# The last linear attention of a four-layer network: chains of taps taken in threes in a fixed order, with the start of a pooled attention beside it

## The chip, the cores and the metric

One core of a Trainium2 chip runs the whole kernel in one launch. The metric is device time in microseconds (us), the median of several executions. One more execution is recorded by the hardware profiler; all durations of single instructions come from that one.

## The reference

The input x is 4 images of 256 channels and 64 x 64 points, in fp32. Four layers follow one another, each `x = x + layer(group_norm(x))`:

```python
# 0: deformable convolution block: 1x1 conv, 3x3 depthwise conv, offsets and masks, bilinear gather of
#    9 points in 4 groups, projection; then squeeze-excite and a feed-forward 256 -> 1024 -> 256
# 1: linear attention
qkv = relu(conv1x1(x, qkv_w) * s + b)                     # 768 channels
agg = depthwise5x5(qkv, agg_dw_w) + ...                   # 25 taps a channel
q, k, v = split(concat([qkv, agg]))                       # in heads of 8
q, k = relu(q), relu(k)
out = (v k^T) q / ((sum k) q + eps)
x = x + relu(conv1x1(out, proj_w) * s + b)
# 2: 3x3 convolution with binarised weights
# 3: attention with keys and values from a 2x2 max pool: softmax(theta^T phi) g, then a 1x1 conv
```

## The kernel before

An image is 2 tiles of 128 channels (KT) by 4096 points, cut into 8 blocks of 512 points (NB). The work is written as Python generators, one for each piece: `feed` (feed-forward), `linear` (layer 1, `layer1`), `conv` (layer 2, `layer2`), `pooled` (layer 3, `layer3`). Each `yield` gives a cost. `beside(steps, number, *works)` runs through a main loop and calls each work so that at every step its spent cost follows a straight line from its share `lo` to its share `hi`; so it writes the instructions of the works interleaved. There are two ways in which that order reaches the engines. Inside `with ordered():` TensorE, VectorE (DVE), ScalarE (ACT) and GpSimd (POOL) get the instructions in the order written. Outside it the framework's scheduler orders them by its own estimates. The DMA queue of SyncE (SP) is left to the scheduler in both.

While the gather of image n runs (`sample`, bound to the four engines in kept order), the feed-forward and linear attention of image n-1 and both last layers of image n-2 go beside it. When the last gather (image 3) is over, three stages are left, all outside `ordered()`:

```python
self.banks, self.alone = cycle(["mm", "acc", "mm", "dp", "mm"]), True
beside(range(64), 64, *behind(N - 1), (conv(N - 2), CONV, 0.2, 1))
self.banks = cycle(["mm", "mm", "mm", "vk"])
beside(range(64), 64, (conv(N - 1, "right"), CONV, 0, 1), (pooled(N - 2, True), SECOND - CONV, 0, 1))
for _ in pooled(N - 1, True): pass
```

`behind(3)` is the feed-forward and then the linear attention of image 3; conv(2) goes beside the latter. Then come conv(3) beside pooled(2), and pooled(3) alone.

**The linear attention.** `rows` makes q, k or v for a block and a tile of channels: a matrix product (L773), ScalarE's relu, and copies into padded buffers (`pad0`, `pad1`) that the 5 x 5 taps read. The tiles are taken in three passes t: two of keys and values, (2, 4) and (3, 5), and one of queries, (0, 1). A chain is 25 taps over 1024 points of one tile; 6 tiles by 4 row groups (NCH) are 24 chains. On VectorE (`depthwise`, L180) each tap is one instruction on an accumulator in PSUM (`agg`). When `alone` is set, chains of which the running number leaves 2 after division by 3 go to `products` instead: ScalarE multiplies (L195, buffers `m`), GpSimd adds (L196). The chains are written one after the other. After every third tap `step` takes one piece from the list `later`: the relu of a finished chain, the transposes and outer products of keys and values (`outer`), the sums over keys (`summed`, kk), and for queries the output: `dens` (denominator, rd), `head` (num, rden, ot; eight for each row group), `proj` (ps, pr, xq; four).

**PSUM** has eight banks of 512 fp32 columns: three `mm`, one each of `acc`, `dp` and `vk`, two of `agg`. `ps()` hands them out in the turn that `banks` says.

**layer2** adds 18 products (36 TensorE instructions, L937) for each block and tile of channels, yields after each three, and adds the result to x (`leave`, L928) after the first three of the next such unit. **layer3** has a preamble over 8 blocks (L988 to L1005) and then 32 iterations, four to a block: scores s (L1022), their maxima (L1023), exponentials (L1029), transposes (L1037, L1038), the product with the values (L1042), scaling (L1043). With `wide` the scores take banks of acc, dp and agg.

Of the kernel before, what the change touches and what calls it, by code (L numbers as in the profile page):

```python
# [9 lines left out]
F32 = mybir.dt.float32  # L10
# [7 lines left out]
P = 128  # L18
N, C, H, W = 4, 256, 64, 64
# [7 lines left out]
NCH = NT // CT  # L27
# [7 lines left out]
LEADS = 12, 14, 16, 18  # L35
# [3 lines left out]

CONVOLVE, OFFSETS, BINARY = NB * 9 + 26, 60, 62  # L40
FEED = NB * 40 + 8
LINEAR = 930
CONV, SECOND = NB * 32 + 2, 631
EPS_BN = 1e-5
EPS_GN = 1e-5
# [25 lines left out]
class Net:  # L71
# [10 lines left out]
    def ps(self, name="ps"):  # L82

        tag = next(self.banks)
        return (self.mm if tag == "mm" else self.ps1).tile([P, 512], F32, name=name, tag=tag)

    def rsqrt(self, pool, v, eps, cols, name):

# [82 lines left out]
    def depthwise(self, acc, src, w, k, rows, cols, r0, bias=None, step=lambda cost: cost, out=None):  # L171


        nc = self.nc
        for t in range(k * k):
            s = src[:, r0 + t // k:r0 + t // k + rows, t % k:t % k + cols]
            wt = w[:, t:t + 1]
            if t:
                to = acc if out is None or t < k * k - 1 else out
                nc.vector.scalar_tensor_tensor(to, s, wt, acc, ALU.mult, ALU.add)  # L180
            elif bias is not None:
                nc.vector.tensor_scalar(acc, s, wt, bias, ALU.mult, ALU.add)
            else:
                nc.vector.tensor_scalar(acc, s, wt, None, ALU.mult)
            if t % 3 == 2 or t == k * k - 1:
                yield step(3.9)

    def products(self, pool, acc, src, w, k, rows, cols, r0, bias, step):

        nc = self.nc  # L190
        for t in range(k * k):
            s = src[:, r0 + t // k:r0 + t // k + rows, t % k:t % k + cols]
            if t:
                m = pool.tile([P, rows, cols], F32, name="m", tag="product", bufs=4)
                nc.scalar.activation(m, s, AF.Copy, scale=w[:, t:t + 1])  # L195
                nc.gpsimd.tensor_tensor(acc, acc, m, ALU.add)  # L196
            else:
                nc.scalar.activation(acc, s, AF.Identity, bias=bias, scale=w[:, t:t + 1])
            if t % 3 == 2 or t == k * k - 1:
                yield step(0.5)  # L200


    def setup(self):
# [514 lines left out]
    def layer1(self, n, st, st2):  # L718
        nc, tc, a = self.nc, self.tc, self.a
        rw = lambda v: v.rearrange("p (r w) -> p r w", w=W)  # L720
        fl = lambda v: v.rearrange("p r w -> p (r w)")
        with tc.tile_pool(name=f"la{n}", bufs=1, side="right") as sp, \
# [11 lines left out]
            ld = sp.tile([P, 4, 64], F32, name="ld")  # L734
            nc.vector.memset(ld, 0.0)

            later, turn, count = [], 0, 0
            room = lambda bufs: bufs + self.alone

            def step(cost, chains=False):  # L740


                nonlocal count
                if later:
                    later.pop(0)()
                if chains:
                    count += 1
                    if count in LEADS:
                        next(made, None)
                return cost  # L750


# [2 lines left out]
            ks = [sp.tile([P, 2, NB], F32, name=f"ks{t}") for t in range(2)]  # L755
            ready = []

            def rows():


                for t, tiles in enumerate(((2, 4), (3, 5), (0, 1))):
                    new = lambda c: [self.padded(bp, 1, 20, 2, c, f"pad{i}", bufs=room(3)) for i in range(2)]
                    pads = {0: new(0)}
                    for b in range(NB):
                        c, h = divmod(b, 2)
                        x = self.block(bp, self.x3_d[n], b, "xr")
                        if h and c + 1 < NCH:
                            pads[c + 1] = new(c + 1)
                        got = []
                        for i, m in enumerate(tiles):  # L770
                            ps = self.ps()
                            for k in range(KT):
                                nc.tensor.matmul(ps, qw[:, k, m * P:(m + 1) * P], x[:, k], start=k == 0, stop=k == KT - 1)  # L773
                            bn = {"bias": qb[:, m:m + 1], "scale": self.vec("qkv_s", m)}
                            dst = {j: p[i][:, 0] for j, p in pads.items()}
                            if t < 2:
                                v = bp.tile([P, 512], F32, name="v", tag=f"v{i}")
                                added = {} if i else {"accum_out": ks[t][:, 0, b:b + 1]}
                                nc.scalar.activation(v, ps, AF.Relu, **bn, **added)  # L779
                                self.spread(dst, rw(v), b, 2)  # L780
                                got.append(v)
                            else:
                                self.spread(dst, None, b, 2, lambda own: nc.scalar.activation(own, rw(ps), AF.Relu, **bn))  # L783
                            if i:
                                if got:
                                    outer(t, 0, *got, t == 0 and b == 0, False)
                                for j in [c - 1] * (b > 0 and not h) + [c] * (b == NB - 1):
                                    ready.append((t, tiles, j, [p[:, 0] for p in pads.pop(j)]))
                            yield

            def aggregate(pd, i, name, relu=True, **more):


                nonlocal turn
                turn += 1
                v = lambda tag, bufs: bp.tile([P, 16, W], F32, name=name, tag=tag, bufs=bufs)
                tick = lambda cost: step(cost, True)
                if self.alone and turn % 3 == 2:
                    out = v("av2", 3)
                    yield from self.products(bp, out, pd, self.w5[:, i], 5, 16, W, 0, self.b5[:, i:i + 1], tick)  # L800
                else:
                    acc, out = self.ps1.tile([P, 16, W], F32, name="agg", tag="agg"), v("ag", room(3))
                    yield from self.depthwise(acc, pd, self.w5[:, i], 5, 16, W, 0, bias=self.b5[:, i:i + 1], step=tick, out=out)
                if relu:
                    later.append(lambda: nc.scalar.activation(out, out, AF.Relu, **more))
                return out

            def outer(t, kind, kv, vv, first, last):

# [74 lines left out]
                for h in range(2):  # L884
                    later.extend([partial(head, h, j) for j in range(4)] + [partial(proj, h, m) for m in range(KT)])

            made = rows()
            for _ in range(3 * NCH):
                while not ready:
                    next(made)  # L890
                    yield step(3)
                t, tiles, c, pd = ready.pop(0)
                count, got = 0, []
                for i, m in enumerate(tiles):
                    more = {} if t == 2 or i else {"accum_out": ks[t][:, 1, c:c + 1]}
                    got.append((yield from aggregate(pd[i], m, ("ak", "av")[i], t == 2 or not i, **more)))
                if t == 2:
                    output(c, pd, got)
                    continue
                outer(t, 1, *map(fl, got), False, c == NCH - 1)  # L900
                if c == NCH - 1:
                    later.append(partial(summed, t))
            while later:
                yield step(4)

# [1 line left out]
    def layer2(self, n, st, st3, side="left"):  # L907
        nc, tc = self.nc, self.tc
        with tc.tile_pool(name=f"ca{n}", bufs=1, side=side) as sp, \
# [5 lines left out]
            for b in range(NB):  # L915
# [15 lines left out]
                        nc.sync.dma_start(self.x5_d[n][:, :, b * 512:(b + 1) * 512], xv)  # L931

                for m in range(KT):
                    ps = self.ps()
                    for i in range(KT * 9):
                        k, t = i // 9, i % 9
                        nc.tensor.matmul(ps, w[:, k, t, m * P:(m + 1) * P], xp[:, k, t // 3:t // 3 + 8, t % 3:t % 3 + W],  # L937
                                         start=i == 0, stop=i == KT * 9 - 1)
                        if i % 3 == 2:
                            if before:  # L940
                                before.pop()()
                            yield 2.7
                    before.append(partial(leave, m, ps, xv, b))
# [109 lines left out]
    def run(self):  # L1053
# [11 lines left out]
        def second(n):  # L1065
            yield from conv(n)
            yield from pooled(n)

        def beside(steps, number, *works):
# [14 lines left out]

            for i, _ in enumerate(steps, 1):
                advance(i / number)
            while open_:
                advance(float("inf"))

        rounds = sum(-(-n_ // RP) for _, n_ in BLOCKS)  # L1090
        E = mybir.EngineType
# [2 lines left out]
        with self.tc.tile_pool(name="gather", bufs=2, side="left") as self.gp, \  # L1094
# [16 lines left out]
            with ordered():  # L1111
                beside(self.sample(1, ssum[1]), rounds, (self.binarise(), BINARY, 0, 0.2), *behind(0))
                for n in range(2, N):
                    beside(self.sample(n, ssum[n]), rounds, *behind(n - 1), (second(n - 2), SECOND, 0.2, 1))
        self.banks, self.alone = cycle(["mm", "acc", "mm", "dp", "mm"]), True
        beside(range(64), 64, *behind(N - 1), (conv(N - 2), CONV, 0.2, 1))

        self.banks = cycle(["mm", "mm", "mm", "vk"])
        beside(range(64), 64, (conv(N - 1, "right"), CONV, 0, 1), (pooled(N - 2, True), SECOND - CONV, 0, 1))
        for _ in pooled(N - 1, True):  # L1120
            pass

# [92 lines left out]
```

## Time and profile before

| | us |
|---|---|
| median of 3 runs | 9327.45 (9320.3 to 9335.84) |
| the profiled execution: its own time | 9288.0 |
| its span (first to last instruction) | 9285.9 |
| feed-forward of image 3 ends (last statistics on VectorE) | 7700.6 |
| first tap of the last linear attention | 7720.6 |
| its last tap | 8513 |
| its last store issued | 8564.9 |
| last product of conv(3) ends | 9079 |

| busy over the span | us | share | instructions |
|---|---|---|---|
| TensorE, products | 6286.0 | 68% | 35252 |
| VectorE | 5026.0 | 54% | 6119 |
| ScalarE | 2188.6 | 24% | 4879 |
| GpSimd | 5063.8 | 55% | 4886 |

The shares are means over stages with different limits. What the change touches lies in the last 1800 us, so the windows there are to be read and not these shares. In the profile's rows a group is named by its line, engine and operation, then output <- inputs; behind the bar stand its busy time, the mean ns of one, the idle time of the engine just before it, and what ended it.

### The profile page before, as it was taken

Reading aid. Unit: us, or ns where it says so; the run is one execution under the profiler, and the core shown is the slowest. Engines: PE = TensorE matmul, PEld = TensorE weight load, DVE = VectorE, ACT = ScalarE, POOL = GpSimd, SP = SyncE. Lnnn points to the kernel's source line nnn. Section 1 sums busy time; section 2 is a strip of 40 time slices with the busy share of each in tenths; the row PEclk is TensorE's granted clock in tenths of the full one; section 3 lists DMA queues with packets and bytes.
Section 4 is the critical chain, followed back from the end, with each engine's and each line's share of the span. In section 5 each row is a group of like instructions: output and inputs, shape, how many; then the busy total and the mean of one; then the engine's idle time right before and its main releaser. Section 6 shows DMA issues by size and latency. Waiting matters only on the chain. (4 is left out here: it accounts for less than half of the span.)

```text
span 9285.9 us, 93043 instructions
## 1 busy us (share of the span) xinstructions
PE 6286.0 (68%) x35252; PEld 3432.4 (37%) x35252; DVE 5026.0 (54%) x6119; ACT 2188.6 (24%) x4879; POOL 5063.8 (55%) x4886
## 2 busy tenths in 40 slices
PE   4354544458544557888876877878768796548999
PEld 2232232234323222344444443434444443323556
DVE  4444443443467677226777762266777625775224
ACT  1111111112211111222222222222222225532224
POOL 1666666566666666666666555666665505742000
PEclk7676666669766677999988889999888898778999
DMA  6455554444433344444443435444433321101211
GB/s 162 125 156 148 141 165 126 129 143 146 136 106 104 111 120 115 139 134 125 125 130 112 120 111 153 130 125 124 133 110 116 104 86 45 33 28 57 62 47 62
DMA packets 819967, 1054.96 MB, mean 114 GB/s; under 512 B 464320, under 2 KB 524864, under 8 KB 817984
## 3 DMA queue, kind: packets, MB, share of 16 engines
q0 software_dynamic: 225024, 614.77, 23.0%
q1 hardware_dynamic: 594496, 434.25, 16.4%
q8 instruction: 279, 4.57, 0.2%
q14 instruction: 168, 1.38, 0.0%
HBM read 880.72 MB, written 167.90 MB: 113 GB/s over the span
## 5 line engine op out<-in xcount | busy, mean ns | idle before, releaser
L579 POOL DMA_INDIRECT g<-tab,sl x4688 | 4610.4, 983 | 2798.2 <-issue 1226.2
L180 DVE SCALAR_TENSOR_TENSOR agg<-pad,vec,agg 128x1024 f32<-128x1024 f32 x2280 | 2934.7, 1287 | 64.9
L586 PE MATMUL acc<-g,wm 128*32 128x128 f32 x18752 | 1011.5, 330 | 2006.7 <-ACT at L591 1362.5
L586 PEld LDWEIGHTS acc<-g,wm 128*32 128x32 f32 x18752 | 553.6, 126 | 2514.4 <-ACT at L591 1564.0
L937 PE MATMUL ps<-xp,w 128*128 128x512 f32 x2304 | 1104.7, 619 | 54.0 <-ACT xp L925 23.8
L570 DVE TENSOR_TENSOR wm<-con,sl 128x1024 f32<-128x1024 f32 (+1 forms) x296 | 358.3, 1211 | 814.2 <-remote 560.9
L611 ACT COPY dT<-dp 64x112 f32<-64x112 f32 x1176 | 286.3, 243 | 1554.5 <-remote 695.8
L937 PEld LDWEIGHTS ps<-xp,w 128*128 128x128 f32 x2304 | 436.9, 198 | 542.6 <-issue 501.8
L704 PE MATMUL ps<-x2f,f 128*128 128x512 f32 x1024 | 506.4, 645 | 8.0 <-ACT f L695 4.0
L169 DVE SCALAR_TENSOR_TENSOR hm<-ps,vec,lk 128x512 f32<-128x512 f32 x256 | 191.0, 751 | 505.9 <-ACT lk L168 411.6
L711 PE MATMUL ps<-hm,f 128*128 128x512 f32 x1024 | 458.5, 602 | 0.0
L773 PE MATMUL ps<-xr,qw 128*128 128x512 f32 x768 | 444.5, 706 | 19.7 <-ACT v L779 11.4
L196 POOL TENSOR_TENSOR av<-av,m 128x1024 f32<-128x1024 f32 x96 | 226.1, 2355 | 409.4 <-DMA xr<-x 320.3
L591 ACT COPY at<-acc 128x256 f32<-128x256 f32 (+1 forms) x588 | 218.3, 371 | 690.1 <-remote 551.5
L619 PE MATMUL po<-dT,ow 128*128 128x224 f32 (+1 forms) x1216 | 321.4, 413 | 66.8 <-issue 32.6
L819 ACT COPY kt<-pt 128x512 f32<-128x512 f32 x256 | 147.8, 585 | 841.7 <-remote 486.8
L196 POOL TENSOR_TENSOR ak<-ak,m 128x1024 f32<-128x1024 f32 x96 | 226.6, 2361 | 181.8 <-ACT m L195 174.6
L168 ACT ACTIVATE lk<-ps,low 128x512 f32<-128x512 f32 x256 | 174.4, 687 | 628.6 <-PE ps L704 461.6
L619 PEld LDWEIGHTS po<-dT,ow 128*128 128x128 f32 x1216 | 261.8, 229 | 131.2 <-issue 80.2
L1022 PE MATMUL s<-ph,th 128*128 128x512 f32 x512 | 281.7, 653 | 30.6 <-ACT pad L783 15.1
L704 PEld LDWEIGHTS ps<-x2f,f 128*128 128x128 f32 x1024 | 201.8, 205 | 258.5 <-issue 241.4
L1042 PEld LDWEIGHTS ps<-gt,pT 128*128 128x128 f32 x2048 | 268.7, 207 | 70.2 <-issue 47.2
(233 smaller groups left out, 7709.1 us busy)
## 6 DMA issues: line engine op xcount, KB each, us to landing
g<-tab,sl POOLq DMA_INDIRECT x4688
x<-x SPq DMA_DIRECT2D x128, 512.0 KB
xr<-x SPq DMA_DIRECT2D x96, 512.0 KB
x<-in_x SPq DMA_DIRECT2D x64, 512.0 KB
tab<-xo SPq DMA_DIRECT2D x512, 64.0 KB
y<-yc SPq DMA_DIRECT2D x32, 512.0 KB
x2f<-x SPq DMA_DIRECT2D x32, 512.0 KB
xyf<-x SPq DMA_DIRECT2D x32, 512.0 KB
```

The source lines that it names most:

```text
L180: nc.vector.scalar_tensor_tensor(to, s, wt, acc, ALU.mult, ALU.add)
L196: nc.gpsimd.tensor_tensor(acc, acc, m, ALU.add)
L570: nc.vector.tensor_tensor(wm[:, 0:nu], self.con("own").unsqueeze(1).unsqueeze(1).to_broadcast(sh), sl[:, r:r + nu, G:].unsqueeze(3).to_bro ...
L579: nc.gpsimd.indirect_dma_start(out=g[:, i, :], out_offset=None, in_=table, in_offset=bass.IndirectOffsetOnAxis(ap=sl.bitcast(I32)[:, r, i: ...
L586: nc.tensor.matmul(acc[32 * i:32 * i + 32, :], wm[:, r4, 4 * i + 2 * x:4 * i + 2 * x + 2, :], g[:, i, x * P:(x + 1) * P], start=x == 0, st ...
L611: nc.scalar.copy(dT[b][hs, :, q0:q0 + m * (v1 - v0)].rearrange("p g (v o) -> p g v o", o=m), dp[u][hs, v0:v1, :, s, 0:m].rearrange("p v g ...
L619: nc.tensor.matmul(po[m][:, 0:np_], self.ow[:, k, m * P:(m + 1) * P], dT[b][:, k, 0:np_], start=k == 0, stop=k == G - 1)
L704: nc.tensor.matmul(ps, f1[:, k, m * P:(m + 1) * P], x2[:, k], start=k == 0, stop=k == KT - 1)
L711: nc.tensor.matmul(ps, f2[:, k, m * P:(m + 1) * P], hm[:, k], start=k == 0, stop=k == 4 * KT - 1)
L773: nc.tensor.matmul(ps, qw[:, k, m * P:(m + 1) * P], x[:, k], start=k == 0, stop=k == KT - 1)
L937: nc.tensor.matmul(ps, w[:, k, t, m * P:(m + 1) * P], xp[:, k, t // 3:t // 3 + 8, t % 3:t % 3 + W], start=i == 0, stop=i == KT * 9 - 1)
L1022: nc.tensor.matmul(s[i], tv[:, 4 * b + j], ph[:, i * 512:(i + 1) * 512], start=True, stop=True)
```

## The change

It leaves the arithmetic as it is. It sets the stages behind the last gather anew:

- The feed-forward and the linear attention of image 3 go into `ordered()`, with 900 steps in place of 64. Beside the linear attention goes `rest`, which is conv(2) and behind it pooled(2) in one generator, at a pace that would end at share 1.46. What is left of it at share 1 (a cost of 240 of 631) goes beside conv(3), outside `ordered()` as before.
- Chains are taken in threes: first and third on VectorE, the second on ScalarE and GpSimd, advanced by one product after every second tap of the others. A tap is one step. `later` gives a piece on every second tap, `rows` one block and tile on every eighth.
- The padded buffers are five for each name instead of four, the buffers `m` three instead of four.
- `banks` stays at `mm` alone (three banks in turn); the units of layer2 take acc and dp in turn (`long`). pooled(2) is no longer `wide`; pooled(3) still is.
- A unit of layer2 leaves after nine products of the next one (i = 8) while `alone` is set.

The core of the diff:

```diff
+    def long(self):
+        return self.ps1.tile([P, 512], F32, name="ps", tag=next(self.idle)) if self.alone else self.ps()
...
-            if t % 3 == 2 or t == k * k - 1:
-                yield step(3.9)
+            if self.alone or t % 3 == 2 or t == k * k - 1:
+                yield step(1.3 if self.alone else 3.9)
...
-                m = pool.tile([P, rows, cols], F32, name="m", tag="product", bufs=4)
+                m = pool.tile([P, rows, cols], F32, name="m", tag="product", bufs=3)
...
-            if t % 3 == 2 or t == k * k - 1:
-                yield step(0.5)
+            yield step(0.5)
...
             def step(cost, chains=False):
                 nonlocal count
-                if later:
+                count += chains
+                if later and (not self.alone or count % 2 or not chains):
                     later.pop(0)()
                 if chains:
-                    count += 1
-                    if count in LEADS:
+                    if count % 8 == 6 if self.alone else count in LEADS:
                         next(made, None)
+                    if count % 2 and aside:
+                        next(aside, None)
                 return cost
...
-                    new = lambda c: [self.padded(bp, 1, 20, 2, c, f"pad{i}", bufs=room(3)) for i in range(2)]
+                    new = lambda c: [self.padded(bp, 1, 20, 2, c, f"pad{i}", bufs=room(3, 2)) for i in range(2)]
...
+            made, number = rows(), 0
+            if self.alone:
+                for _ in range(8):
+                    next(made)
+                    yield step(1)
...
+            while number < 6 * NCH:
+                count = 0 if not self.alone and number % 2 == 0 else count
+                *args, more = yield from chain()
+                if self.alone:
+                    *slow, smore = yield from chain()
+                    aside = products(*slow, **smore)
+                    yield from aggregate(*args, **more)
+                    *args, more = yield from chain()
+                    yield from aggregate(*args, **more)
+                    while next(aside, None):
+                        pass
+                    number += 3
...
-                    ps = self.ps()
+                    ps = self.long()
...
-                            if before:
+                            if before and (i > 5 or not self.alone):
                                 before.pop()()
...
-        self.banks, self.alone = cycle(["mm", "acc", "mm", "dp", "mm"]), True
-        beside(range(64), 64, *behind(N - 1), (conv(N - 2), CONV, 0.2, 1))
+        self.idle, self.alone = cycle(["acc", "dp"]), True
+        rest = second(N - 2)
+        with ordered():
+            beside(range(STEPS), STEPS, (feed(N - 1), FEED, 0, 0.27), (linear(N - 1), LAST, 0.27, 1), (rest, SECOND, 0.27, 1.46))
+        beside(range(STEPS), STEPS, (conv(N - 1, "right"), CONV, 0, 1), (rest, 240, 0, 1))
 
         self.banks = cycle(["mm", "mm", "mm", "vk"])
-        beside(range(64), 64, (conv(N - 1, "right"), CONV, 0, 1), (pooled(N - 2, True), SECOND - CONV, 0, 1))
```

`STEPS` is 900 and `LAST` 620. `beside` now ends when every work with a `hi` of at most 1 is done. `aggregate` is split into `aggregate` (VectorE), `products` and `end`, and the pairing of two chains' results is done in `chains`.

More of the change, by code (lines that the diff above doesn't have):

```diff
@@ L41 @@
 FEED = NB * 40 + 8
-LINEAR = 930
+LINEAR, LAST = 930, 620
+STEPS = 900
 CONV, SECOND = NB * 32 + 2, 631
@@ L735, in layer1 @@
             nc.vector.memset(ld, 0.0)
-            later, turn, count = [], 0, 0
-            room = lambda bufs: bufs + self.alone
+            later, count, aside = [], 0, None
+            room = lambda bufs, more=1: bufs + more * self.alone
             def step(cost, chains=False):
                 nonlocal count
-                if later:
+                count += chains
+                if later and (not self.alone or count % 2 or not chains):
                     later.pop(0)()
                 if chains:
-                    count += 1
-                    if count in LEADS:
+                    if count % 8 == 6 if self.alone else count in LEADS:
                         next(made, None)
+                    if count % 2 and aside:
+                        next(aside, None)
                 return cost
@@ L789, in rows, with aggregate, products, end @@
                             yield
[L791 to L803, printed above, removed]
+            def aggregate(pd, i, name, done, relu=True, **more):
+                acc = self.ps1.tile([P, 16, W], F32, name="agg", tag="agg")
+                out = bp.tile([P, 16, W], F32, name=name, tag="ag", bufs=room(3))
+                yield from self.depthwise(acc, pd, self.w5[:, i], 5, 16, W, 0, bias=self.b5[:, i:i + 1],
+                                          step=lambda cost: step(cost, True), out=out)
+                end(out, done, relu, **more)
+            def products(pd, i, name, done, relu=True, **more):
+                out = bp.tile([P, 16, W], F32, name=name, tag="av2", bufs=3)
+                yield from self.products(bp, out, pd, self.w5[:, i], 5, 16, W, 0, self.b5[:, i:i + 1], lambda cost: cost)
+                end(out, done, relu, **more)
+            def end(out, done, relu, **more):
                 if relu:
                     later.append(lambda: nc.scalar.activation(out, out, AF.Relu, **more))
-                return out
+                done(out)
             def outer(t, kind, kv, vv, first, last):
@@ L885, in output, with chains, done @@
                     later.extend([partial(head, h, j) for j in range(4)] + [partial(proj, h, m) for m in range(KT)])
-            made = rows()
-            for _ in range(3 * NCH):
-                while not ready:
+            def chains():
+                for _ in range(3 * NCH):
+                    while not ready:
+                        next(made)
+                        yield None
+                    t, tiles, c, pd = ready.pop(0)
+                    got = {}
+                    def done(i, v, t=t, c=c, pd=pd, got=got):
+                        got[i] = v
+                        if len(got) < 2:
+                            return
+                        if t == 2:
+                            return output(c, pd, [got[0], got[1]])
+                        outer(t, 1, fl(got[0]), fl(got[1]), False, c == NCH - 1)
+                        if c == NCH - 1:
+                            later.append(partial(summed, t))
+                    for i, m in enumerate(tiles):
+                        more = {} if t == 2 or i else {"accum_out": ks[t][:, 1, c:c + 1]}
+                        yield pd[i], m, ("ak", "av")[i], partial(done, i), t == 2 or not i, more
@@ L890, in layer1, with chain @@
+            made, number = rows(), 0
+            if self.alone:
+                for _ in range(8):
                     next(made)
+                    yield step(1)
+            every = chains()
+            def chain():
+                while not (args := next(every)):
                     yield step(3)
[L892 to L902, printed above, removed]
+                return args
+            while number < 6 * NCH:
[10 more added lines that the diff above has]
+                    number += 3
+                else:
+                    yield from aggregate(*args, **more)
+                    number += 1
@@ L1086, in beside @@
                 advance(i / number)
-            while open_:
-                advance(float("inf"))
+            while any(works[j][3] <= 1 for j in open_):
+                advance(1)
         rounds = sum(-(-n_ // RP) for _, n_ in BLOCKS)
```

## The prediction

> **What bounds the kernel now.** I read the slices of the span first, then windows over the stretch in which the work of the last image stands alone, then the waits of VectorE in it, then the groups of instructions by shape.
>
> ```profile
> PE   4354544458544557888876877878768796548999
> ...
> DVE  4444443443467677226777762266777625775224
> ...
> POOL 1666666566666666666666555666665505742000
> PEclk7676666669766677999988889999888898778999
> ```
>
> GpSimd is busy in every slice until the 33rd; that is mostly the gather, which the change does not touch. What follows it, from 7465 us, is touched. Windows over it (columns: length, busy us and instructions of TensorE, its weight loads, VectorE, ScalarE, GpSimd; granted TensorE clock; DMA share; GB/s):
>
> ```profile
> 7705.00:7865.00 160.00, 105.09 (x343) 57.00 (x343) 96.95 (x123) 94.55 (x128) 109.42 (x47) 0.80 0.15 46
> 7865.00:8025.00 160.00, 87.16 (x313) 51.34 (x313) 117.21 (x116) 91.91 (x123) 111.99 (x48) 0.76 0.11 31
> 8025.00:8185.00 160.00, 94.51 (x295) 50.80 (x295) 125.33 (x116) 74.73 (x94) 95.86 (x41) 0.78 0.15 41
> 8185.00:8345.00 160.00, 67.28 (x139) 26.19 (x140) 108.04 (x98) 55.88 (x64) 78.26 (x34) 0.64 0.04 13
> 8345.00:8513.00 168.00, 124.72 (x257) 45.29 (x256) 124.51 (x120) 53.72 (x64) 57.15 (x24) 0.84 0.14 42
> ...
> 8568.00:9070.00 502.00, 495.70 (x1764) 279.01 (x1763) 126.38 (x329) 121.20 (x252) 0.00 (x0) 0.99 0.21 62
> 9070.00:9286.00 216.00, 200.33 (x1062) 149.83 (x1060) 95.94 (x255) 103.28 (x232) 0.00 (x0) 0.97 0.20 66
> ```
>
> From 7705 to 8513 (the last linear attention beside conv(2)) no engine is full: VectorE 572 of 808 us, 71%. From 8568 TensorE is full. So a gain can come from the gaps in the first stretch, and from moving TensorE work out of the second into them. Who made VectorE wait from 7720 to 8560 (us in total, times, longest):
>
> ```profile
> DVE pad L436 <- ACT m L195: 79.1, 5, 20.9
> DVE rd L856 <- PE den L854: 59.1, 4, 28.4
> DVE x L928 <- PE ps L937: 36.0, 5, 12.8
> DVE kk L841 <- ACT ak L805: 23.3, 1, 23.3
> DVE xq L878 <- ACT pr L877: 17.6, 10, 3.1
> DVE ot L869 <- PE rden L866: 17.1, 18, 2.1
> ```
>
> With smaller ones it is 240 us: the scheduler put instructions into VectorE's queue ahead of what they need.
>
> The prices, by shape, in the same stretch:
>
> ```profile
> L180 DVE SCALAR_TENSOR_TENSOR agg<-pad,vec,agg 128x1024 f32<-128x1024 f32 x368 | 472.9, 1285 | 8.7
> ...
> L196 POOL TENSOR_TENSOR av<-av,m 128x1024 f32<-128x1024 f32 x96 | 226.1, 2355 | 409.4 <-DMA xr<-x 320.3 <-ACT m L195 81.9
> L195 ACT ACTIVATE m<-pad,vec 128x1024 f32<-128x1024 f32 x192 | 219.4, 1158 | 147.0 <-POOL ak L196 78.0 <-POOL av L196 68.9
> ```
>
> A full-width TensorE instruction (128x512) costs 0.43 us when TensorE is full: the chain of waits has 174 of L937 in 74.70 us.
>
> **What the Trainium skill says.** "PSUM — Partial Sum Buffer", Engine vs sequencer instructions: ScalarE, VectorE and GpSimd are strict first-in-first-out queues, and matmuls keep program order too. The trace agrees: while VectorE waited 28.4 us for den it ran none of its ready taps. "TensorE: Matmul & The Clock Gate", What's actually happening: the array's clock is throttled unless TensorE was recently busy. The trace agrees in the mean: 0.64 where it was busy 42%, 0.99 where it was 99%. "SBUF — State Buffer", SBUF: two separate sides: a VectorE operation with two SBUF inputs can block GpSimd. Here the taps read one input from PSUM, and they last 1207 to 1293 ns with GpSimd running or not, so I charge nothing.
>
> **The change, part by part.** Up to the last feed-forward both built programs have the same instruction order on every engine; GpSimd's is the same to the end. I charge zero up to 7699 us. The feed-forward keeps its TensorE order and loses two of five PSUM banks in turn: a bank is held for 1.72 (four instructions) + 0.69 (ScalarE) + 0.75 us (VectorE), 3.2 us, over three banks 1.1 us each, under TensorE's 1.72. Zero; without that cover, at most 64 times a few tenths, 20 us.
>
> *Start of the chains.* Before, the first tap starts at 7720.6. Now a second group norm, an xp scaling (two of 0.9 us) and four rows stand ahead of it on ScalarE: +6 us, 7727.
>
> *The chains.* There were 16 chains on VectorE and 8 on ScalarE/GpSimd; this stays. An aside chain now advances one product per two taps: GpSimd needs 24 x 2.36 = 57 us, two VectorE chains 64 us, so it is hidden, and so are ScalarE's 24 x 1.16. VectorE's sum for the stretch:
> - 16 chains of 1.34 + 23 x 1.285 + 1.28: 515
> - heads 32 x 0.69, rd 4 x (0.69 + 3.35), xq and its statistics 16 x 1.44: 61
> - conv(2) leaving 16 x 1.37: 22
> - pad memsets, sums, small norms: 17
> - newly here: pooled(2)'s preamble 8 x 1.40 + 3, and by the order 7 of its 32 iterations at 2.26 (two maxima of 0.69, one scaling of 0.35, small ones), one output: 31.
>
> 646 us; 33 of it stand behind the last chain, 10 ahead of the first: 603 remain.
>
> *Waits that go.* Pads: by the order a buffer is asked for again only when its chain, counted in taps, is over (five buffers instead of four): 79 to 0. A unit of conv(2) leaves two yields later (i = 8), behind nine products of the next (7.7 us of TensorE) instead of three: 36 to 0. kk 23 to 0. The den wait gets shorter, not zero.
>
> *Waits that stay.* In kept order rd stands two taps behind its den, head and projection directly behind their TensorE work. Behind each waits the next tap. The stretch from 6700 to 7440, also in kept order, has the prices: rd 15.2 us in 3, xq 24.4 in 9, ot 42.4 over 32 heads. Three rd, 10 xq, 22 heads lie ahead of the chains' end: 15 + 27 + 29 = 71. In the first eleven VectorE chains TensorE is given some 340 us of full-rate work (88% of conv(2)'s 576 x 0.43: 217; rows 34 x 1.72; transposes and outer products 62, at 0.13 us an instruction) in 384 us of VectorE's: 0.9. Below full clock it falls behind now and then: I take 15 us, between 0 and 70. So 603 + 86: last tap at 8416 (before: 8513).
>
> *Behind the chains.* 18 steps are left: den 6.9, ten heads x 1.72, six projections x 3.44, 5.5 pooled iterations x 4.8 (below), one output 1.7: 73 us of TensorE; at a clock of 0.9, 81, plus waits, 95 (80 to 125). End of the linear attention 8511 (before: 8564).
>
> *Conv(3).* TensorE's second stretch loses 174 instructions of conv(2) (75 us), the preamble (27) and 7 iterations. The preamble is 8 x (4 x 0.43 + 8 x 0.13) + 5. An iteration is (516 - 322 - 27 - 14) / 32 = 4.8 us: the stretch of before (8563 to 9079) less 750 x 0.43, preamble and eight outputs. It gains a hole: conv(3)'s weights (w, 2304 KB) are loaded only when the linear attention's buffers are free, as before (issue at 8568.1, 3 us behind the last store), some 25 us to its first matmul; then conv(2) filled it, now 1.5 iterations. 25 + 247 + 23.5 x 4.8 + 12 = 397; pooled(2) now has three banks and no wide ones, for which I add 11 (0 to 40): 408, to 8919 (before: 515).
>
> *Pooled(3)* has the same banks and order: 207 us as before (9079 to 9286). 9126.
>
> SP: its loads follow their buffers; xq and x5 loads stand behind stores that wait for VectorE, as before; no charge, bounded by the 40 us above.
>
> Sum: span 9285.9 to 9126, -160 (97 from the chains' end, less 44 for the longer tail behind them, 107 from conv(3)'s stretch). The profiled execution took 9288.0, 39 below the median of the runs, 9327.45; I take the same difference from the median: 9167, call it 9170.
>
> **Rivals.**
> 1. *TensorE paces the chains.* At the 0.78 granted now, 340 us become 436, 52 over VectorE's 384; with the tail at 125 it is 82 more, with the bank cost at 20 too 91: 9260. For it: the 0.9 above, and stops of TensorE at transposes (87.5 us behind av before). Against: the clock rose with use in every window.
> 2. *Almost no waits.* Waits at 30, tail 80, no bank cost: 56 + 15 + 11 less: 9090. For it: heads are prepared one ahead where a bank is free.
> 3. *Slower: head-of-line waits.* 32 heads, 16 projections, 4 rd, 16 leaves, 7 iterations of three joints: some 90 joints at which kept order stops VectorE with all taps behind. The forecast has 0.8 us at each; it turns to a loss from 160 us more, 2.6 us at each. At 3.3 us: 9390. Against: 6700 to 7440 shows 1 to 5 us only at the output's joints, with more on TensorE.
> 4. *Nothing moves*: pooled(2) stays in conv(3)'s stretch and the gaps stay. The built order speaks against it: 7 iterations stand ahead of the last linear statistics.
>
> **How the numbers follow.** Forecast 0.66 (9120 to 9225 of its own), first rival 0.15, second 0.12, third 0.05, fourth 0.02. Range 9090 to 9270: 9090 is the second rival, 9270 just over the first. About 0.2%, 19 us, is what a measurement of this kernel can tell from no change. Faster by more 0.92, within 0.03, slower 0.05.
>
> **What would show it.** Right: last tap near 8416; pad, kk and conv-leave waits of VectorE near zero, rd some 5 us each; VectorE over 85% busy between; first conv(3) matmul 20 to 30 us behind the last xq store; conv(3)'s stretch near 408. Wrong: taps in even gaps before the first den (TensorE paces), granted clock under 0.85 there, or a second stretch above 440.

## The result and the profile after

The changed kernel takes 9096.77 us (median of 4 runs, 9089.74 to 9110.71), the kernel before 9327.53 us beside it: ratio 0.9754, 95% interval 0.9737 to 0.9771, 231 us less. The forecast was 9170, 157 less: the direction was right and the gain 74 us larger than forecast. The time lies 7 us inside the range (9090 to 9270) and outside the band to which the forecast itself gave most of its chance, 9120 to 9225.

The profiled execution took 9094.8 us, span 9092.7, only 193 us under that of before. The other 38 us are in the gather part, which both kernels have alike: its last add in the feed-forward ended at 7738.1 us here and at 7699.8 before. From there to the end it is 1354.6 us after and 1586.1 before, 231.5 less, which agrees with the medians. So from here on I measure from the first tap of the last linear attention, not from zero.

The slices of the span:

```profile
PE   3354444448644447788876677888866879987999
...
DVE  4444443443466667324667774236677752898324
...
POOL 1666666556666666666666655666666540685000
PEclk7666666669766667798988888999988889998999
```

GpSimd's last part is denser (6, 8, 5 where before it was 5, 7, 4, 2), and VectorE has 8, 9, 8 where it had 5, 7, 7, 5. The windows, cut at the first tap, the last tap, the last xq store, the first conv(3) matmul and the end of conv(3) (columns as before):

```profile
7763.60:8425.00 661.40, 557.28 (x1613) 265.35 (x1611) 610.15 (x608) 371.71 (x490) 454.83 (x192) 0.91 0.17 50
8425.00:8506.00 81.00, 72.31 (x245) 37.47 (x244) 28.58 (x53) 25.77 (x49) 0.00 (x0) 0.98 0.12 39
8506.00:8523.00 17.00, 12.24 (x58) 10.41 (x59) 7.01 (x31) 9.98 (x18) 0.00 (x0) 0.80 0.93 274
8523.00:8884.00 361.00, 361.00 (x1262) 203.44 (x1262) 82.82 (x199) 82.51 (x171) 0.00 (x0) 1.00 0.17 49
8884.00:9092.70 208.70, 195.00 (x1055) 148.16 (x1053) 97.32 (x259) 103.29 (x232) 0.00 (x0) 0.98 0.21 69
```

VectorE is now busy 610 of 661 us, 92%, against 570 of 793 before, and TensorE 557, against 465. The granted clock is 0.91 where it was 0.76. "TensorE: Matmul & The Clock Gate", What's actually happening, in the Trainium skill has the clock throttled unless TensorE was recently busy. These means agree: 84% busy at 0.91 and 59% at 0.76. Added up from the first tap to the end, TensorE does the same work (1198 us busy, before 1213) in 1329 us instead of 1565. Its gaps went from 352 to 131 us, and that is 221 of the 236 us gained there.

Who made VectorE wait between first and last tap (us in total, times, longest; the first line ends where the first tap begins):

```profile
DVE agg L187 <- ACT pad L451: 13.0, 1, 13.0
DVE ln L847 <- PE vk L831: 9.4, 1, 9.4
DVE xq L886 <- ACT pr L885: 9.0, 6, 3.5
DVE ot L877 <- PE rden L874: 8.0, 6, 3.2
DVE rd L864 <- PE den L862: 4.1, 2, 2.5
DVE mx L1067 <- PE s L1066: 2.2, 2, 1.3
...
DVE x L972 <- PE ps L981: 0.8, 1, 0.8
```

The pad waits (79 us before) and those for key maps (kk, 23) are gone. The wait for the denominators fell from 59 (53 of it up to the last tap) to 4, and that for conv(2)'s tiles from 36 (26 up to the last tap) to under 1. The prices did not move (groups by shape, same stretch):

```profile
L185 DVE SCALAR_TENSOR_TENSOR agg<-pad,vec,agg 128x1024 f32<-128x1024 f32 x368 | 473.3, 1286 | 10.7
...
L201 POOL TENSOR_TENSOR av<-av,m 128x1024 f32<-128x1024 f32 x96 | 227.3, 2367 | 419.0 <-ACT m L200 413.3
L200 ACT ACTIVATE m<-pad,vec 128x1024 f32<-128x1024 f32 x192 | 218.1, 1156 | 22.9 <-POOL av L201 16.9 <-POOL ak L201 5.9
```

Before, they were 1285, 2355 and 1158 ns. What changed is how long ScalarE's products wait for GpSimd: 147.0 us before, 22.9 now.

### The profile page after: what moved, and what is told of

Same layout as the page of the kernel before. It is cut to its first block, busy times and chain, and to the rows that moved or that the text cites. A ratio compares the mean times of both kernels' runs of the same rounds, so it can differ in the third digit from the quotient of the medians.

```text
span 9092.7 us, 92982 instructions
## 1 busy us (share of the span) xinstructions
PE 6276.0 (69%) x35252; PEld 3446.3 (38%) x35252; DVE 5043.6 (55%) x6119; ACT 2185.0 (24%) x4881; POOL 5072.1 (56%) x4886
## 5 line engine op out<-in xcount | busy, mean ns | idle before, releaser
L981 PE MATMUL ps<-xp,w 128*128 128x512 f32 x2304 | 1123.6, 628 | 80.8 <-ACT xp L969 41.1
L1086 PE MATMUL ps<-gt,pT 128*128 128x128 f32 x2048 | 283.1, 297 | 13.3 <-issue 12.0
```

Source lines behind the costliest of these rows:

```text
L1086: nc.tensor.matmul(ps[:, 0:P], pT[:, m], gt[:, m], start=m == 0, stop=m == 7)
```

## The experiments

All are made from the changed kernel. Beside each ratio to the kernel before stands the time from the first tap to the end in the profile of the run. That number is much steadier than the whole: a second profile of the changed kernel (the eighth run) gave 1329.2, the first 1329.05, while the gather part ahead of it differed by 67 us. Every other kernel has one profile, so differences of a few us rest on this one repeat. Stages, in us (the xq store by the start of its issue):

| kernel | ratio, 95% interval | first to last tap | to last xq store | to end of conv(3) | to end | sum |
|---|---|---|---|---|---|---|
| before | 1 | 793 | 51 | 514 | 207 | 1565 |
| changed | 0.9754 (0.9737–0.9771) | 661 | 80 | 378 | 209 | 1329 |
| free order | 0.9906 (0.9884–0.9929) | 807 | 81 | 377 | 208 | 1474 |
| no pooled beside | 0.9765 (0.9745–0.9784) | 626 | 80 | 446 | 204 | 1356 |
| neither | 0.9931 (0.9914–0.9947) | 810 | 51 | 437 | 204 | 1503 |
| early leave | 0.9765 (0.9735–0.9794) | 672 | 80 | 378 | 209 | 1340 |
| side chain in a burst | 1.0099 (1.0078–1.012) | 992 | 72 | 381 | 209 | 1655 |
| four pads | 0.9763 (0.9741–0.9786) | 663 | 87 | 378 | 208 | 1336 |
| side chain each tap | 0.9896 (0.9874–0.9918) | 787 | 72 | 377 | 209 | 1445 |
| more pooled (to 1.20) | 0.976 (0.9741–0.9779) | 728 | 90 | 330 | 204 | 1351 |
| changed, again | 0.9754 (0.9735–0.9774) | 662 | 80 | 378 | 209 | 1329 |
| some more pooled (to 1.30) | one run | 688 | 86 | 350 | 204 | 1328 |
| less pooled (to 1.70) | one run | 634 | 70 | 379 | 256 | 1339 |

**1. Free order.** The last linear stage without the kept order:

```diff
-        with ordered():
-            beside(range(STEPS), STEPS, (feed(N - 1), ...
+        beside(range(STEPS), STEPS, (feed(N - 1), ...
```

> The changed kernel without the kept order in its last linear stage: the same calls in threes, single taps, five pads, pooled(2) begun beside it, but the scheduler orders the queues. If the kept order is what takes VectorE's 240 us of waits away: waits of the old kind come back, last tap 60 to 120 us later behind the feed-forward, 9150 to 9220. If the written pace (threes, one product per two taps) does it and the order follows from it anyway: within 20 us of the changed kernel, 9080 to 9120.

Measured: 145 us longer than the changed kernel from the first tap on, all of it between first and last tap (807 against 661); every later stage is as in the changed kernel. Waits of VectorE of the old kind are back (between first and last tap):

```profile
DVE x L972 <- PE ps L981: 82.9, 8, 31.6
DVE kk L849 <- ACT ak L813: 32.2, 2, 25.4
DVE pad L440 <- ACT m L200: 30.7, 3, 15.1
DVE kk L849 <- ACT v L785: 17.7, 2, 16.5
```

The longest of each kind takes 15 to 32 us: the scheduler puts an instruction into VectorE's queue long ahead of what it needs.

**2. No pooled attention beside the linear one.** `(rest, SECOND, 0.27, 1.46)` becomes `(conv(N - 2), CONV, 0.27, 1)`, and pooled(2) stands wholly beside conv(3). The edit also slows conv(2), which now ends with the linear attention and not well before it.

> The changed kernel with pooled(2) wholly beside conv(3), only conv(2) beside the linear attention. By the sum of the prediction: the chains lose 31 us of VectorE (about 15 ahead of the last tap), the tail loses its iterations (some 20 us), conv(3)'s stretch gains the preamble 27 and 7 x 4.45 us: in all 15 to 45 us slower, 9110 to 9140. Rival: the pooled work lay in free gaps only and all of its 60 us comes back: 9150 to 9165. Rival: it had cost the linear stage as much as it gave: within 10 us.

Measured: the whole times can't tell it from the changed kernel; from the first tap on it is 27 us longer. The chains are 35 us shorter and conv(3)'s stretch is 68 longer. The 27 us are not the pooled work alone: 85 of conv(2)'s 576 TensorE instructions now stand behind the last tap, where the changed kernel has none.

**3. Conv(2)'s results leave early**, as before the change:

```diff
-                            if before and (i > 5 or not self.alone):
+                            if before:
```

> The changed kernel with a unit of conv(2) leaving behind three products of the next unit (i = 2), as before, instead of nine. If VectorE is stopped by a TensorE that runs behind in the first eleven chains: some 2 us at each of 14 leaves, 10 to 40 us slower, and a row of waits of x for ps of some 20 to 40 us. If TensorE keeps level: no change (within 10 us).

Measured: 11 us longer in the chains, nothing elsewhere; VectorE's wait for conv(2)'s tiles is 10.5 us there instead of 0.8. So the late leave is worth about 10 us, and it removed the smaller part of the 26 us of these waits up to the last tap.

**4. The side chain in a burst.** All 25 products of the ScalarE/GpSimd chain are written at once, at the start of each group of three chains:

```diff
                     aside = products(*slow, **smore)
+                    while next(aside, None):
+                        pass
```

> The changed kernel with the 25 products of an aside chain written at once at the start of its three, instead of one per two taps. If the even pace matters: ScalarE's queue is shut for the 57 us that GpSimd takes, rows, relus and kt behind it come late, TensorE stops, and VectorE at the next leave or pad: 60 to 200 us slower. If ScalarE's lead is enough: within 15 us.

Measured: slower than before; the chains take 992 us. Waits of all engines between first and last tap:

```profile
DVE x L974 <- PE ps L983: 235.9, 5, 55.6
...
PE vk L831 <- ACT kt L827: 154.5, 15, 53.1
...
PE ps L983 <- ACT xp L971: 99.2, 6, 55.1
```

Behind 24 products in ScalarE's queue stand the copies of the transposed keys (kt) and conv(2)'s scaled inputs (xp). Each burst lasts as long as GpSimd needs, about 55 us; TensorE waits for ScalarE that long, and VectorE, with its taps behind the conv(2) tile, waits for TensorE. This is the mechanism of the forecast's third rival, waits at the head of a queue with ready work behind, here brought about by the order alone. It fits "PSUM — Partial Sum Buffer", Engine vs sequencer instructions, in the Trainium skill: the queues of ScalarE, VectorE and GpSimd are strictly first in, first out.

**5. Four pads instead of five**: `room(3, 2)` becomes `room(3, 1)`.

> The changed kernel with four buffers in turn for each padded tile of the last linear attention instead of five. Theory of the forecast (the fifth buffer is what takes VectorE's waits at the pads away): a pad is asked for while the side chain that reads its predecessor still has products ahead of it, so VectorE, in kept order, waits for ScalarE and GpSimd at the pads, 40 to 80 us in all between first and last tap, all of it on the path: 40 to 80 us longer than the changed kernel. Rival (the kept order and the even pace of the side chain took the waits away, the fifth buffer is spare): pads under 20 us, time within 20 us.

Measured: 7 us longer, VectorE's wait at the pads 5.6 us. The forecast gave the order and the fifth buffer together as its reason. In kept order the fifth buffer is nearly spare; without it, five buffers still left 30.7 us of pad waits (run 1). So it is mainly the order that takes the waits away.

**6. The side chain at every tap** instead of every second one: `if count % 2 and aside:` becomes `if aside:`.

> The changed kernel, but the side chain on ScalarE and GpSimd is written down one product per tap of VectorE instead of one per two. Theory (the pace written must fit what GpSimd can do: 2.37 us a product against 1.29 a tap): with three product buffers ScalarE stops at every product until GpSimd has added the one three before, so whatever stands behind on ScalarE (key transposes, scaled inputs of conv(2), head outputs) is up to half a chain late; TensorE waits for it, and VectorE for TensorE; the side chains are over after 25 taps and GpSimd then idles. 60 to 200 us longer than the changed kernel, with VectorE's waits for the conv(2) tiles and the denominators grown. Rival (only a burst hurts, the engines even out a pace that is off by a factor of two): within 25 us.

Measured: 115 us longer, all in the chains. Waits of all engines there:

```profile
DVE x L972 <- PE ps L981: 110.9, 8, 29.8
...
ACT m L200 <- POOL ak L201: 71.8, 62, 1.6
...
PE ps L981 <- ACT xp L969: 60.1, 7, 26.9
ACT m L200 <- POOL av L201: 58.8, 52, 1.3
```

ScalarE stops 114 times for GpSimd, 131 us in all. One product per tap, 1.29 us, is written faster than GpSimd adds one (2.37 us). One per two taps, 2.58 us, fits.

**7. More of pooled(2) beside the chains**: the share's end 1.46 becomes 1.20, and 11.5 iterations stand ahead of the last tap instead of 2.

> The changed kernel with more of the second pooled attention beside the last linear attention (its share of the steps ends at 1.20 instead of 1.46). Theory (VectorE and TensorE each have what the other stretch lacks, so an iteration moved costs VectorE 2.3 us beside the chains and saves TensorE 4.45 us behind them): with about 7 iterations more, 16 us longer chains against 31 us less behind them, 10 to 20 us shorter than the changed kernel. Rival (the chains lose to kept order what conv(3)'s stretch gains: beginning it beside was itself worth nothing that the first experiments could tell): within 8 us either way, or up to 20 us longer, with VectorE's waits for TensorE grown by the same sum.

Measured: 22 us longer. The chains grow by 66 us, VectorE's busy time in them only by 26 (636 against 610), TensorE's by 51. That is about 7 us for each of the 9.5 iterations, more than their work on either engine, and each saves about 5 behind the chains. But the same number sets conv(2)'s pace: its last product came 383 us after the first tap instead of 458, and VectorE's wait for its tiles rose from 0.8 to 33.9 us, half of the 66. So the 7 us are not the price of an iteration alone; what it would be at conv(2)'s old pace was not tried.

**8. The changed kernel again**, on the same chip as runs 5 to 7.

> The changed kernel itself, on the same chip as the three others, as their base: 225 to 240 us shorter than before, a ratio of 0.974 to 0.977. A second profile of one program also says how far its stages vary by themselves: the linear stage and what follows within 10 us of the first profile, the gather ahead of them by up to 40.

Measured: every stage within 1 us of the first profile.

**9. Neither part**: runs 1 and 2 together.

> Neither part: the changed kernel without the kept order in its last linear stage and with the second pooled attention wholly beside conv(3); what is left is the new arrangement of chains by single taps. It closes a square with the runs that left out one part each. From the first tap to the end the changed kernel took 1329 us in both of its profiles, the free order 1474, the kept order without pooled beside it 1356, the kernel before 1565. If the two parts are independent: 1474 + 27, so about 1500, near 0.993 of before, and the new arrangement by itself is worth some 65 us. If pooled work beside is worth more under a free scheduler, which can put it into gaps: 1520 to 1565. If it is in the scheduler's way: under 1480.

Measured: 1503, so the parts are nearly independent. The kept order is worth 145 us with pooled(2) beside it and 147 without. Pooled(2) beside, with the pace of conv(2) that goes with it, is worth 27 in kept order and 30 in free order. What is left, 62 us, is everything else in the change together; the whole times, 63 us apart, agree. Those 62 us are not in the chains, which take 810 us against 793. They are in conv(3)'s stretch (437 against 514): conv(2), of which 174 instructions, 75 us, stood there before, is now wholly beside the linear attention. Which of the other edits brought that about was not tried.

**10 and 11. Two more shares of pooled(2)**, ending at 1.30 and at 1.70.

> The share of the second pooled attention ends at 1.30, between the changed kernel's 1.46 and the 1.20 that put 11.5 iterations ahead of the last tap instead of 2. Theory (an iteration among the chains costs them 7 us and saves 5 us behind them): the total from first tap to end lies between, 1335 to 1348 us. Rival (there is a best share between the two): under 1325.

> The share of the second pooled attention ends at 1.70, so fewer iterations stand in the 80 us behind the last tap. Theory (that stretch is set by the chain from denominators to outputs, and pooled work in it is free): it stays 78 to 82 us long, conv(3)'s stretch grows by 4.5 us an iteration, and the total from first tap to end is 1333 to 1345 us. Rival (TensorE sets it): it shortens by what is taken out and the total stays within 3 us of 1329.

Measured: 1328 at 1.30, between what the theory and its rival said. With 7 iterations ahead of the last tap, 32 us more in the chains and behind them go with 33 us less in conv(3)'s stretch and the last one.

At 1.70 the sum is 1339, as the theory had it, but not for its reason. Behind the chains no iteration is left, and seven of the eight blocks of pooled(2)'s preamble stand there instead; the stretch shrinks from 80 to 70 us, with TensorE busy 67 of 70, so TensorE sets it and not a chain of waits. Conv(3)'s stretch does not grow either. The cost of 240 that sets pooled(2)'s pace beside conv(3) was left as it was, so six iterations no longer fit there and run behind conv(3): the last stage takes 256 us, where it is 204 with nothing of pooled(2) in it. Beside conv(3), at the 4.3 us an iteration costs there (next section), they would take about 31 us and not 52. By that estimate 1.70 with the 240 raised comes to some 1320 us, a little under the changed kernel; no run tried it.

Between 1.46 and 1.30 the sum is flat (1329 and 1328), and it is longer at 1.20 (1351). No version run here is clearly faster than the changed kernel.

## Why the prediction was right, and 74 us short

By its own steps, from the first tap to the end; the forecast's 1399 us stand against 1329. The mechanism held: VectorE's old waits went, and work of TensorE's second stretch moved into the gaps of the first. The sizes did not, and the time is inside the range by 7 us only.

- *Feed-forward at zero cost, first tap:* right. From the last gather to the end of the feed-forward it is 288 us, before 290. From there to the first tap 25.6 us (forecast 27, before 20.9).
- *VectorE's sum between the taps:* 603 forecast, 610 measured.
- *Waits that go* (138 us): right in size. The reasons given were not all right: the pads went by the order, with little need of the fifth buffer (runs 1 and 5), and the late leave is worth about 10 us of the 36 (run 3). The order does most of it (run 1).
- *Waits that stay:* **the largest wrong term**, 86 forecast. VectorE's whole idle time, 661 − 610, is 51 us, with small gaps of 0.03 us at each tap in it. I had priced the joints at what they cost in the gather part: rd 15, xq 27, ot 29. They cost 4, 9 and 8. The other 15 us, for TensorE falling behind, were not needed: that wait is 0.8 us. The mean clock of 0.91 does not explain the cheap joints. From the first denominator (8194.9 us) to the last tap, where they stand, the clock was 0.83, no higher than the 0.85 of the stretch that gave the prices; in run 2 it was 0.90 there, and they cost 35 us instead of 21. Why they cost so little stays open. First to last tap 661, not 689.
- *Behind the chains:* 95 forecast, 80 measured. TensorE is busy 72.3 us there (73 forecast, with 5.5 iterations of pooled(2) where four to five came). The clock was 0.98, not 0.9, which is most of the difference, and the waits beside it were 8 us, not 14.
- *Conv(3)'s stretch:* 408 forecast, 378 measured. The hole is 17 us, not 25 (timeline: the last store of xq, the load of w, and from the chain of waits the first conv(3) matmuls):

```profile
8505.15 0.56 SPq L889 DMA_DIRECT2D x<-xq  x1
...
8508.29 0.33 SPq L956 DMA_DIRECT2D w<-w  x1
```

```profile
8522.46 7.81 PE ps L981 x18
```

  Then TensorE is busy 361 of 361 us. Less conv(3)'s 247 and 10 for six outputs, 24 iterations (48 maxima on VectorE) take 104 us, 4.3 each, not 4.8. The 4.8 came from a stretch in which TensorE was busy 507 of 514 us, so it held gaps, but these are only 0.2 us an iteration; the rest is not shown. No cost of having three banks shows (11 forecast).
- *Pooled(3):* 207 forecast, 209 measured.

The errors, 28 + 15 + 30 − 2, are the 70 us by which the stretch was shorter, all on one side. The second rival (almost no waits, 9090), to which I gave 0.12, came nearest. The first rival, TensorE pacing the chains, fell: up to the first denominator TensorE was busy 90% at a clock of 0.95. (Its price held twice the 15 us that the forecast already had for TensorE: 9245, not 9260.) The third did not occur at the written pace, but runs 4 and 6 show that it is the danger of the kept order: at twice the pace it takes back 115 of the 236 us, and in a burst more than all.

## What to carry to other kernels

In this kernel an order written by hand beat the scheduler's where several in-order queues feed each other, but only with the side chain written at a pace that its slowest engine could keep: one product per two taps gained, where one per tap and a burst lost 115 and 325 us against it. Prices of instructions carried over from one stretch to another within 1%; prices of waits did not (21 us at the joints where 71 were forecast). When a share of moved work is tried at several values, look whether the same number moves anything else: here it set conv(2)'s pace as well, and the 240 behind it had to go with it. Measure from a fixed event, not by the whole time, when what stands ahead of it is less steady.

## What the runs showed of the hardware

The gather part is far less steady than what follows it. In runs 5 to 8 its last issue on GpSimd came at 7379 to 7415 us. In runs 9 to 11, in a later session and by the record on the same chip, it came at 6378 to 6385 us, and the kernel before took 8255.21 us there instead of 9274.36. A gather instruction's median duration was 946 to 949 ns in both; the time between them differed. What made the gather part faster was not tried and stays open.

No kernel has a profile in both sessions. But pooled(3), with nothing of pooled(2) beside it, took 203.8 and 203.9 us in runs 2 and 7 and 204.4 in runs 9 and 10. That is why runs 9 to 11 are compared with the others from the first tap on.
